# Order of leaf sums, scales and turns, and idle TensorE products, in a fused conditioned block of two layer pairs

## The chip, the cores and the metric

The kernel runs on one core of one Trainium2 chip. Its engines are TensorE (PE in the profile; its weight loads are PEld), VectorE (DVE), ScalarE (ACT), GpSimd (POOL) and SyncE (SP), which issues most DMAs. Each engine works through its own queue in program order and waits on semaphores for the others. The metric is the device time of one execution in microseconds (us). The kernel before takes 595.75 us, the median of three runs (595.74 to 597.34).

## The reference

x has 2 batches of 2048 rows of 512 columns, all float32. Cut to what matters:

```python
emb = silu(t) @ ada_w + ada_b
shift_msa, scale_msa, gate_msa, shift_mlp, scale_mlp, gate_mlp = split(emb, 6)
norm = ln(x) * (1 + scale_msa) + shift_msa
h = gelu(norm @ ssm_w1 + ssm_b1)            # 512 -> 512
x = x + gate_msa * (h @ ssm_w2 + ssm_b2)    # 512 -> 512
norm2 = ln(x) * (1 + scale_mlp) + shift_mlp
hf = gelu_tanh(norm2 @ ff_w1 + ff_b1)       # 512 -> 1024
x = x + gate_mlp * (hf @ ff_w2 + ff_b2)     # 1024 -> 512
```

ln takes mean and variance over the 512 columns. The shifts, scales and gates are one row per batch.

## The kernel before

The 4096 rows are cut into eight blocks of 512 rows, i = 0 to 7; four blocks make a batch. A block passes through four matrix products, named by their tiles: hA (first layer, `First`), oA (its residual, `residual`), hC (feed-forward layer, `Second`), oC (its residual, `residual_in_leaves` for i from 1 on). Everything is float32, in which a product of TensorE runs as two passes. A product of two matrices cut into quarters is made of seven quarter products instead of eight, from sums of quarters that VectorE and GpSimd form ahead (P1 to P7, taken in the order P1, P2, P6, P5, P7, P3, P4); hC from i=1 on takes 26 products from a table (`HK_P`), whose right operands are 20 forms of the normalised block, made by the list `HK_B` into the tile `forms`; and in oC some of the seven are split again into "leaves", seven rounds r = 0 to 6 of small products, whose operands are the leaf sums sums24, sums35 and sums7 of hC's output (`leaf_sums`, each four sums in the line L348). VectorE adds each round's result from PSUM into x (L795) before the banks are used two rounds on. "five" is true in all blocks but 1 and 4: then five of the seven go by leaves (P2, P3, P4, P5, P7) and P1 and P6 are plain; otherwise three do (P2, P3, P4).

The order of all work is written by hand. Each product takes a dictionary of hooks: `hook(hooks, places, ops)` puts operations behind a place, and they are emitted there, in the order of hooking. Places of hC are the numbers 0 to 25 of its products; places of hA and oA are P1 to P7; places of oC are P1 and P2 behind plain products (in a five block P2 lies behind the plain P6), and for a five block P6, P5, R2, P7, (R4, P3), P4 behind rounds 1, 2, 3, 4, 5, 6. In the others P1, P2, P6 lie behind the plain P1, P5, P6, and P5, R2, P7, R4, P3, P4 behind rounds 1 to 6. Where an operation stands among the hooks sets its place in its engine's queue, not a time.

A norm (`Norm`; n1 ahead of hA, n2 ahead of hC) goes through these steps: `stats` (VectorE, L508); `scales` (L513), which makes 1/sqrt and the scaled mean of four values a row in eight small steps on GpSimd, or, with on_dve, the first two there (L517, L519, a power of -0.5) and four on VectorE (L525 to L528); `normal` (ScalarE, L549); `turn` (VectorE, L560, transposes within 32 by 32); `move` (16 DMAs of 64 KB, L569, on SP or on SP and ScalarE's queue by halves); `moved`, the modulation by scale and shift (ScalarE, L592, or another engine, L594); then the forms (L870).

While hC of block i runs, x of block i+1 is loaded a second time (`load_x(i + 1)`), since its first copy was normalised in place; its buffer is that of a block whose store must be done. The loop at L1216 emits for block i: hC_i; oA of i+1; oC_i with n2 of i+1 hooked into it; then hA of i+2. `nxt` and `nx2` say that i+1 and i+2 exist, `last` is i = 7. In block 4, `leaf_fold` holds sums that remake the leaf weights for the second batch.

At the start five idle products of 512 columns (L1026) run on the identity while the first loads land, then rows_of(0) (L275), 32 small products for the shift rows, once ada_0 has landed, and rows_of(1) once ada_1 has; then 16 transposes of the first normalised block (L578) and their modulation (L592, L594), and the first layer of block 0.

Of the kernel before, what the change touches and what calls it, by code (L numbers as in the profile page):

```python
# [83 lines left out]
HK_B = [  # L84
    (23, '-', 4, 6),
    (22, '-', 0, 23),
    (21, '+', 1, 3),
    (20, '-', 21, 22),
    (19, '-', 7, 21),
    (18, '-', 5, 21),  # L90
    (17, '+', 3, 23),
    (16, '-', 18, 23),
# [48 lines left out]
def kernel(  # L141
# [16 lines left out]
    nc = tc.nc  # L158
    P = 128
# [4 lines left out]
    C = 4  # L164
# [22 lines left out]
    IDLE = 5  # L187
# [5 lines left out]
    ROWS = R_FB1 + KH  # L193
    def big_tile(name):
        return big.tile([P, KD, D], F32, tag="big", name=name)
# [3 lines left out]
    def load_x(i, pieces=1):  # L199
        xs[i] = big_tile(f"x_{i}")  # L200
        for s in range(pieces):
            c = slice(s * C // pieces, (s + 1) * C // pieces)
            nc.sync.dma_start(out=xs[i][:, c, :], in_=x_blk[i][:, c, :])
# [29 lines left out]
    rows = brows[:ROWS, 2, :P]  # L233
# [5 lines left out]
    ident = const.tile([P, P], F32, tag="ident", name="ident")  # L239
# [29 lines left out]
    def rows_of(g):  # L269

        pa = ps_g.tile([P, D], F32, tag="x", name=f"pada_{g}")
        w = ada[g].rearrange("p k (n m q) -> p k m n q", n=KD, q=G)
        for k in range(KD):
            for m in range(P // G):
                nc.tensor.matmul(  # L275
                    pa[m * G : (m + 1) * G, :P],
                    silu[:, k, :],
                    w[:, k, m],
                    start=(k == 0),
                    stop=(k == KD - 1),  # L280
                    tile_position=(0, m * G),
                    skip_group_check=True,
                )
        return pa

    def modulation(g0, part):

        g = g0 + part
        pa = rows_of(g)
        turned = pa[:, P : 2 * P]  # L290
        nc.vector.transpose(turned, pa[:, :P])
        turned = turned.rearrange("p (n q) -> p n q", n=KD)
        m = const.tile([P, KD, B], F32, tag=f"mod_{g0}_{part}", name=f"mod_{g0}_{part}")
        bias = colsT[:, R_ADA + g * KD : R_ADA + (g + 1) * KD]
        nc.vector.tensor_tensor(m, turned[:, :, :B], bias.unsqueeze(2).to_broadcast([P, KD, B]), ALU.add)
        mods[g0, part] = m
# [80 lines left out]
    def weight_of_first(name, w_sb):  # L377

        K, M = w_sb.shape[1], w_sb.shape[2]
        tile_s = const.tile([P, 3, K // 2, M // 2], F32, tag=f"{name}_s", name=f"{name}_s")  # L380
        s = thirds(tile_s)
        lo, hi = w_sb[:, : K // 2, :], w_sb[:, K // 2 :, :]
        q = quarters(lo, hi, slice(0, M // 2), slice(M // 2, M))
        return first_operands(q, s), sums_of_first(q, s, nc.gpsimd), tile_s
# [28 lines left out]
    def leaves_of_weight(w_sb, s, engs):  # L413


        def views(w):
            v = w.rearrange("p (h k) (q e d) -> p h k q e d", h=2, e=2, d=P)
            return {f"{h + 1}{e + 1}": v[:, h, :, :, e, :] for h in range(2) for e in range(2)}

        lo, hi = w_sb[:, : w_sb.shape[1] // 2, :], w_sb[:, w_sb.shape[1] // 2 :, :]  # L420
        q23, t23 = views(hi), thirds(pair_t)
        o23 = second_operands(q23, t23)
        ops = {p: {n: v[:, :, j, :] for n, v in o23.items()} for j, p in enumerate(("P2", "P3"))}
        sums = {"P23": sums_of_second(q23, t23, engs["P23"])}
        for j, (p, w) in enumerate((("P4", s[:, 2]), ("P5", s[:, 0]), ("P7", lo[:, :, D // 2 :]))):
            q, t = {n: v[:, :, 0, :] for n, v in views(w).items()}, thirds(fw2_t[:, 2 + j])
            ops[p] = second_operands(q, t)
            sums[p] = sums_of_second(q, t, engs[p])
        return ops, sums
# [59 lines left out]
    def hook(hooks, places, ops):  # L489

        for n, op in enumerate(ops):
            hooks.setdefault(places[min(n, len(places) - 1)], []).append(op)
# [369 lines left out]
    def sums_of_registers(program, reg, engs):  # L862


        def op(n, d, f, a, b):
            eng = engs[n % len(engs)]
            if f == "n":
                nc.vector.scalar_tensor_tensor(reg[d], reg[a], -1.0, reg[b], ALU.mult, ALU.subtract)
            else:
                eng.tensor_tensor(reg[d], reg[a], reg[b], ALU.add if f == "+" else ALU.subtract)  # L870

        return [lambda z=(n,) + step: op(*z) for n, step in enumerate(program)]
# [128 lines left out]
    def run(ops):  # L1001
        for op in ops:
            op()
# [4 lines left out]
    n1 = {0: Norm(0, 1), 1: Norm(1, 1)}  # L1008
# [9 lines left out]
    pt = ps_t.tile([P, 512], F32, tag="t", name="rowsT")  # L1018
# [1 line left out]
    fb1T = colsT[:, R_FB1:ROWS]  # L1020

    idle = ps_g.tile([P, C, P], F32, tag="v", name="idle")
    for n in range(IDLE):
        if n == IDLE - 1:
            nc.tensor.transpose(pt[:, :ROWS], rows, ident[:ROWS, :ROWS])
        nc.tensor.matmul(  # L1026
            idle, ident, ident.unsqueeze(1).to_broadcast([P, C, P]), start=True, stop=True
        )

    run(n1[0].stats())  # L1030
    nc.vector.tensor_copy(colsT, pt[:, :ROWS])
# [18 lines left out]
    w1_ops, w1_sums, _ = weight_of_first("w1", w1_sb)  # L1050
    run(w1_sums)
    modulation(0, 0)
    for c in range(C):
        n1[0].normal(c, nc.vector if c % 2 else None, on_pe=True)
    modulation(0, 1)
# [14 lines left out]
    gb, hA = {2: b2_bc}, {}  # L1070
# [12 lines left out]
    hooks = {}  # L1083
# [12 lines left out]
    hooks = {}  # L1096
# [4 lines left out]
    n2 = {0: Norm(0, 2)}  # L1101
# [21 lines left out]
    hooks = {}  # L1123
# [19 lines left out]
    hooks = {}  # L1143
# [8 lines left out]
    turns = [lambda c=c: n1[2].turn(c) for c in range(C)]  # L1152
# [5 lines left out]
    hooks = {}  # L1158
# [25 lines left out]
    hooks = {}  # L1184
# [10 lines left out]
    hooks = {}  # L1195
# [7 lines left out]
    hooks = {}  # L1203
# [12 lines left out]
    for i in range(1, NBLK):  # L1216
        five = i % PER_B != (1 if i < PER_B else 0)
        nxt, nx2, last = i + 1 < NBLK, i + 2 < NBLK, i + 1 == NBLK
        hC = Second(i)
        hooks = {}  # L1220
        if i == 1:
            hook(hooks, range(0, 26), take(len(fa_sums)))
        if i == 1:
            engs = {"P23": nc.gpsimd, "P4": nc.gpsimd, "P5": nc.vector, "P7": nc.vector}
            leaf_wops, ops = leaves_of_weight(fw2_sb, fw2_s, engs)
# [6 lines left out]
            hook(hooks, (0, 1, 3, 5, 7), later)  # L1232
            later = []
        if nxt:
            hook(hooks, (0,), [lambda: load_x(i + 1)])
            hook(hooks, (1, 2, 3, 4), hA[i + 1].summed(nc.gpsimd))
        if nx2 and i > 1:
            hook(hooks, (5,) if five else (9,), [n1[i + 2].scales])
# [19 lines left out]
        hooks = {}  # L1258
        hook(hooks, EARLY, hC.summed(1, nc.gpsimd if nxt else nc.vector))
        engs = (nc.gpsimd, nc.gpsimd, nc.gpsimd if nx2 else nc.vector)  # L1260
        sums24, sums35, sums7 = hC.leaf_sums(nxt, nx2, five, engs)
        hook(hooks, ("P5",), sums24)
        if last or not five:
            hook(hooks, ("P7",), sums35)
        else:
            hook(hooks, ("P7",) if nx2 else ("P5", "P7", "P7", "P3"), sums7)
        if nxt:

# [11 lines left out]
        leaf_fold, fold = fold and fold[11:], None  # L1280

        hooks = {}
# [6 lines left out]
            hook(hooks, ("P2",), [lambda: apart_leaves(gb[5], nc.gpsimd)])  # L1289
        if nxt:  # L1290

            hook(hooks, ("P1",), [lambda: n2[i + 1].scales(on_dve=not nx2)])
            if five:
                hook(hooks, ("P1",), sums35)
            hook(hooks, ("P1",), [lambda c=c: n2[i + 1].normal(c) for c in range(C)])
            turns = (("P6",) if leaf_fold else ("P2",) if five else ("P2", "P2", "P6")) if nx2 else ("P1",)
            if leaf_fold:
                hook(hooks, ("P1", "P1", "P2", "P2"), leaf_fold)
            hook(hooks, turns, [lambda c=c: n2[i + 1].turn(c) for c in range(C)])
            hook(hooks, turns[-1:], [lambda: n2[i + 1].move((nc.sync, nc.scalar))])  # L1300
# [5 lines left out]
        if nx2:  # L1306
            hook(hooks, ("P1", "P2"), n1[i + 2].summed(nc.gpsimd))
        if nxt:
            moved = n2[i + 1].moved((None,) if nx2 else (None, nc.vector))
            hook(hooks, ("R2",) if nx2 else ("P5", "R2", "P5", "R2"), moved)  # L1310
        refold5 = (i + 1) % PER_B == 0 and nxt
        if not last and not refold5:
# [4 lines left out]
        if nxt:  # L1317
            late = {}

            def form(engs):  # L1320

                fb[i + 1] = n2[i + 1].registers()
                return sums_of_registers(HK_B, fb[i + 1], engs)

            if not nx2:

                def late_form(n):
                    if n == 0:
                        late["ops"] = form((nc.vector,) * 4 + (nc.gpsimd,) * 16)
                    late["ops"][n]()  # L1330

                hook(hooks, ("R2",), [lambda n=n: late_form(n) for n in range(len(HK_B))])

        residual_in_leaves(f"oC_{i}", i, hC, fw2_ops, leaf_wops, KH // 2, hooks, last, five)
        if refold5:
# [8 lines left out]
        if refold5:  # L1344
            take_gate(5, b)
            fw2_ops, fold = weight_of_second(fw2_sb, fw2_s, gate[5, b], (nc.vector,))
            leaf_wops, ops = leaves_of_weight(fw2_sb, fw2_s, dict.fromkeys(("P23", "P4", "P5", "P7"), nc.vector))
            fold += ops["P23"] + ops["P4"]
            later = ops["P5"] + ops["P7"]
        hooks = {}  # L1350
# [13 lines left out]
            unread_stats = st[2:] if refold5 else []  # L1364
            hook(hooks, ("P7", "P4") if refold5 else ("P5", "P7", "P3", "P4"), st[:2] if refold5 else st)
        if nx2:
            hA[i + 2] = First(i + 2, n1[i + 2].ops, hooks, on_act=("P6", "P5"))


# [43 lines left out]
```

## Time and profile before

| | us |
|---|---|
| runs | 595.74, 595.75, 597.34 |
| profiled execution, its own time | 597.37 |
| its span, first to last instruction | 595.2 |
| TensorE busy | 581.6 (98%), 3247 instructions |
| TensorE's weight loads busy | 517.2 (87%) |
| VectorE busy | 434.5 (73%) |
| GpSimd busy | 424.2 (71%) |
| ScalarE busy | 244.7 (41%) |
| mean granted TensorE clock | 0.994 of full |

A busy engine is one that executes; TensorE's weight loads lie beside its products. Where stages are named by time: block 0 up to 133, then per block hC, oA, oC and the next hA, some 69 us in all; hC_4 begins at 342.6, oC_4 at 377.4, hC_6 at 483.1, oC_6 at 517.6, hC_7 at 544.7, oC_7 at 567.2; TensorE ends at 590.6.

### The profile page before, as it was taken

To read this page: it belongs to the slowest core of one execution; us is meant where nothing else is said; L and a number is where in the kernel's file an instruction comes from. 1 tells how busy PE (TensorE), PEld (TensorE's weight loads), DVE (VectorE), ACT (ScalarE), POOL (GpSimd) and SP (SyncE) were. 2 spreads that over 40 slices of the span, in tenths; PEclk is the share of its full clock that TensorE was granted. 3 is DMA by queue.
4 is the path that set the end of the run, shared out by engine and by line. 5 is a ranking of instruction groups with operands and counts; after the bars stand their busy time and mean duration, and the time that the engine had idled before them with its cause. 6 is when DMAs were issued, how large, how long until landed. Compare 5 with 4: busy or idle time off the path is not lost.

```text
span 595.2 us, 9335 instructions
## 1 busy us (share of the span) xinstructions
PE 581.6 (98%) x3247; PEld 517.2 (87%) x3247; DVE 434.5 (73%) x784; ACT 244.7 (41%) x425; POOL 424.2 (71%) x503
## 2 busy tenths in 40 slices
PE   7999999999999999999999999999999999989996
PEld 4888888887889888998889988888889988879886
DVE  4879788996665685786757688756857636788686
ACT  2235357405632454444733457135554346112420
POOL 2676359999982958969697869948689773645470
PEclk9999999999999999999999999999999999989999
DMA  8990323302205303452034711144021500022002
GB/s 318 395 380 5 90 63 84 103 36 106 56 17 149 153 0 77 123 181 81 10 81 131 247 48 40 33 117 166 2 66 26 155 38 1 0 47 97 1 1 72
DMA packets 25243, 56.49 MB, mean 95 GB/s; under 512 B 4672, under 2 KB 5740, under 8 KB 23532
## 3 DMA queue, kind: packets, MB, share of 16 engines
q1 hardware_dynamic: 21472, 51.15, 26.6%
q10 hardware_dynamic: 3724, 4.75, 3.3%
q8 instruction: 26, 0.43, 0.3%
q14 instruction: 21, 0.17, 0.1%
HBM read 32.80 MB, written 8.40 MB: 69 GB/s over the span
## 4 chain that ended last, share of the span: by engine, by line
PE 78%; DVE 9%; POOL 5%; issue 3%; DMA 2%; ACT 1%; SPq 0%; DVEq 0%; POOLq 0%; ACTq 0%
PE py_hA L474 9%; PE px_hC L932 8%; PE py_oA L474 8%; PE pv_hC L932 7%; PE py_hC L932 7%; PE pl_oC_P_y L781 6%; PE py_oC L735 6%; PE pv_hA L474 4%; PE pl_oC_P_v L781 4%; PE pv_oA L474 4%; PE py_hC L474 2%; PE px_hA L474 2%; PE px_oA L474 2%; PE pl_oC_P_x L781 2%; DMA ada<-in_L_cond_ada_w_dram 2%
## 5 line engine op out<-in xcount | busy, mean ns | idle before, releaser
L348 POOL TENSOR_TENSOR hSC<-hClo,hChi 128x512 f32<-128x512 f32 (+1 forms) x17 | 20.6, 1215 | 40.3 <-ACT hChi L927 20.5
L508 DVE BATCH_NORM_STATS2 st<-x 128x6 f32<-128x512 f32 x64 | 43.3, 677 | 5.2 <-DMA x<-in_x_dram 5.0
L592 ACT ACTIVATE nT<-nT,mod,mod 128x512 f32<-128x512 f32 x30 | 22.0, 803 | 56.3 <-DMA nT<-blocks 42.4
L870 POOL TENSOR_TENSOR forms<-forms 128x256 f32<-128x256 f32 x55 | 41.4, 752 | 3.2
L932 PE MATMUL py_hC<-forms,fw 128*128 128x256 f32 x168 | 40.8, 379 | 0.0
L870 POOL TENSOR_TENSOR forms<-nT,forms 128x256 f32<-128x256 f32 x41 | 30.1, 757 | 13.6 <-DVE forms L870 13.1
L549 ACT ACTIVATE nT<-x,nmr,rstd 128x512 f32<-128x512 f32 x32 | 23.4, 803 | 39.7 <-POOL nmr L535 30.6
L949 DVE TENSOR_TENSOR hClo<-hClo,py_hC 128x512 f32<-128x512 f32 x42 | 28.5, 684 | 15.3 <-ACT hClo L946 9.5
L932 PEld LDWEIGHTS py_hC<-forms,fw 128*128 128x128 f32 x168 | 31.9, 190 | 4.4
L697 DVE TENSOR_TENSOR x<-py_oA,x 128x512 f32<-128x512 f32 x32 | 22.0, 687 | 18.1 <-PE py_oA L474 17.5
L795 DVE TENSOR_TENSOR x<-pl_oC_P_y,x 128x256 f32<-128x256 f32 (+1 forms) x76 | 28.0, 370 | 9.4 <-PE pl_oC_P_y L781 7.6
L735 PE MATMUL py_oC<-fw,hClo 128*128 128x256 f32 x144 | 33.6, 379 | 0.0
L592 ACT ACTIVATE x<-x,mod,mod 128x512 f32<-128x512 f32 x24 | 17.6, 802 | 38.8 <-DMA x<-blocks 38.8
L870 POOL TENSOR_TENSOR forms<-nT 128x256 f32<-128x256 f32 x12 | 9.1, 756 | 30.8 <-DMA x<-in_x_dram 18.8
L735 PEld LDWEIGHTS py_oC<-fw,hClo 128*128 128x128 f32 x144 | 26.8, 190 | 3.3
L949 DVE TENSOR_TENSOR hChi<-hChi,pv_hC 128x512 f32<-128x512 f32 x35 | 23.2, 680 | 7.0 <-PE pv_hC L932 6.9
L927 ACT ACTIVATE hClo<-hClo,colsT 128x256 f32<-128x256 f32 x56 | 25.3, 499 | 6.3 <-DVE hClo L949 6.0
L932 PE MATMUL px_hC<-forms,fw 128*128 128x256 f32 x112 | 27.6, 379 | 0.0
L474 PE MATMUL py_oA<-w,hA 128*128 128x256 f32 x112 | 26.5, 379 | 0.0
L946 ACT ACTIVATE hClo<-px_hC 128x512 f32<-128x512 f32 x21 | 12.5, 597 | 33.1 <-PE px_hC L932 22.3
L735 PE MATMUL py_oC<-fw_s,hSC 128*128 128x256 f32 x112 | 25.4, 380 | 0.6 <-DVE x L746 0.6
L927 ACT ACTIVATE hChi<-hChi,colsT 128x256 f32<-128x256 f32 x56 | 25.1, 496 | 1.9 <-DVE hChi L949 1.9
(330 smaller groups left out, 1750.5 us busy)
## 6 DMA issues: line engine op xcount, KB each, us to landing
x<-in_x_dram SPq DMA_DIRECT2D x13, 1024.0 KB
out_dram<-x SPq DMA_DIRECT2D x14, 512.0 KB
ada<-in_L_cond_ada_w_dram SPq DMA_DIRECT2D x6, 1024.0 KB
x<-blocks SPq DMA_DIRECT2D x96, 64.0 KB
nT<-blocks SPq DMA_DIRECT2D x72, 64.0 KB
fw<-in_L_cond_ff_w_dram SPq DMA_DIRECT2D x2, 2048.0 KB
nT<-blocks ACTq DMA_DIRECT2D x56, 64.0 KB
w<-in_L_cond_ssm_w_dram SPq DMA_DIRECT2D x3, 1024.0 KB
```

The lines of the kernel that those rows point to most:

```text
L474: nc.tensor.matmul(ps[b][j * apart][:, j, :], lhs(p, j, k), rhs(p, j, k), start=(fresh and j * (not apart) == 0 and k == 0), stop=(p in (" ...
L508: nc.vector.bn_stats(st, xs[self.i][:, c, :])
L549: nc.scalar.activation(t, x_c, AF.Identity, bias=self.nmr[:, c : c + 1], scale=self.rstd[:, c : c + 1])
L592: nc.scalar.activation(dst, src, AF.Identity, bias=shift, scale=scale)
L697: nc.vector.tensor_tensor(d, ps[BANK[p]][:, js], d, ALU.add)
L735: yield lambda j=j, k=k: nc.tensor.matmul(ps[BANK[p]][:, j, :], hops(p, j, k), wops[p][:, k, :], start=False, stop=(k == kdim - 1), skip_g ...
L781: nc.tensor.matmul(t[:, n, :], hops.leaves[p][f][:, k, :], leaf_wops[p][f][:, k, :], start=room not in started, stop=(f in ("P2", "P3", "P ...
L795: nc.vector.tensor_tensor(d, src, d, ALU.add)
L870: eng.tensor_tensor(reg[d], reg[a], reg[b], ALU.add if f == "+" else ALU.subtract)
L927: nc.scalar.activation(h, h, AF.Gelu_apprx_tanh, bias=fb1T[:, m : m + 1])
L932: nc.tensor.matmul(ps[b][:, j, :], fa[ra][:, j * P : (j + 1) * P], fb[rb].rearrange("p a (c q) -> p c a q", q=Q), start=(fresh and j == 0) ...
L949: nc.vector.tensor_tensor(dest(d), dest(d), ps[b], op)
```

## The change

Six edits in one diff. In the loop:

- **Leaf sums and scales.** In blocks 1 and 4 sums35 moves from P7 of oA to P1 of oC, behind the scales of the next norm. In block 6 the scales are made on GpSimd alone. In the last block sums35 is emitted ahead of sums24.
- **Turns.** In block 4 the four transposes and the 16 DMAs behind them move from P6 to P5 of oC; in block 6 from P1 to P2.
- **Modulation and forms of block 7** (emitted in block 6): two of the four modulations go from VectorE to GpSimd; the forms are hooked at P7 instead of R2, and VectorE makes six of the 20 instead of four.
- **Second load of x**: behind product 3 of hC instead of product 0.
- **First reads of hA**: in blocks 1 and 4 the first reads of P6 and P5 go from ScalarE to VectorE.

At the start the idle products get a helper, `warm`; one product of 128 columns is added behind the five, and three of 256 columns between rows_of(0) and rows_of(1).

```diff
@@ -1020,12 +1020,20 @@
     fb1T = colsT[:, R_FB1:ROWS]
 
     idle = ps_g.tile([P, C, P], F32, tag="v", name="idle")
-    for n in range(IDLE):
-        if n == IDLE - 1:
-            nc.tensor.transpose(pt[:, :ROWS], rows, ident[:ROWS, :ROWS])
-        nc.tensor.matmul(
-            idle, ident, ident.unsqueeze(1).to_broadcast([P, C, P]), start=True, stop=True
-        )
+    def warm(count, blocks=2):
+        for _ in range(count):
+            nc.tensor.matmul(
+                idle[:, :blocks],
+                ident,
+                ident.unsqueeze(1).to_broadcast([P, blocks, P]),
+                start=True,
+                stop=True,
+            )
+
+    warm(IDLE - 1, C)
+    nc.tensor.transpose(pt[:, :ROWS], rows, ident[:ROWS, :ROWS])
+    warm(1, C)
+    warm(1, 1)
 
     run(n1[0].stats())
     nc.vector.tensor_copy(colsT, pt[:, :ROWS])
@@ -1050,6 +1058,7 @@
     w1_ops, w1_sums, _ = weight_of_first("w1", w1_sb)
     run(w1_sums)
     modulation(0, 0)
+    warm(3)
     for c in range(C):
         n1[0].normal(c, nc.vector if c % 2 else None, on_pe=True)
     modulation(0, 1)
@@ -1232,7 +1241,7 @@
             hook(hooks, (0, 1, 3, 5, 7), later)
             later = []
         if nxt:
-            hook(hooks, (0,), [lambda: load_x(i + 1)])
+            hook(hooks, (3,), [lambda: load_x(i + 1)])
             hook(hooks, (1, 2, 3, 4), hA[i + 1].summed(nc.gpsimd))
         if nx2 and i > 1:
             hook(hooks, (5,) if five else (9,), [n1[i + 2].scales])
@@ -1259,10 +1268,10 @@
         hook(hooks, EARLY, hC.summed(1, nc.gpsimd if nxt else nc.vector))
         engs = (nc.gpsimd, nc.gpsimd, nc.gpsimd if nx2 else nc.vector)
         sums24, sums35, sums7 = hC.leaf_sums(nxt, nx2, five, engs)
+        if last:
+            hook(hooks, ("P5",), sums35)
         hook(hooks, ("P5",), sums24)
-        if last or not five:
-            hook(hooks, ("P7",), sums35)
-        else:
+        if five and not last:
             hook(hooks, ("P7",) if nx2 else ("P5", "P7", "P7", "P3"), sums7)
         if nxt:
 
@@ -1289,11 +1298,10 @@
             hook(hooks, ("P2",), [lambda: apart_leaves(gb[5], nc.gpsimd)])
         if nxt:
 
-            hook(hooks, ("P1",), [lambda: n2[i + 1].scales(on_dve=not nx2)])
-            if five:
-                hook(hooks, ("P1",), sums35)
+            hook(hooks, ("P1",), [lambda: n2[i + 1].scales()])
+            hook(hooks, ("P1",), sums35)
             hook(hooks, ("P1",), [lambda c=c: n2[i + 1].normal(c) for c in range(C)])
-            turns = (("P6",) if leaf_fold else ("P2",) if five else ("P2", "P2", "P6")) if nx2 else ("P1",)
+            turns = ("P5",) if leaf_fold else ("P2",) if five else ("P2", "P2", "P6")
             if leaf_fold:
                 hook(hooks, ("P1", "P1", "P2", "P2"), leaf_fold)
             hook(hooks, turns, [lambda c=c: n2[i + 1].turn(c) for c in range(C)])
@@ -1306,7 +1314,7 @@
         if nx2:
             hook(hooks, ("P1", "P2"), n1[i + 2].summed(nc.gpsimd))
         if nxt:
-            moved = n2[i + 1].moved((None,) if nx2 else (None, nc.vector))
+            moved = n2[i + 1].moved((None,) if nx2 else (None, nc.gpsimd))
             hook(hooks, ("R2",) if nx2 else ("P5", "R2", "P5", "R2"), moved)
         refold5 = (i + 1) % PER_B == 0 and nxt
         if not last and not refold5:
@@ -1326,10 +1334,10 @@
 
                 def late_form(n):
                     if n == 0:
-                        late["ops"] = form((nc.vector,) * 4 + (nc.gpsimd,) * 16)
+                        late["ops"] = form((nc.vector,) * 6 + (nc.gpsimd,) * 14)
                     late["ops"][n]()
 
-                hook(hooks, ("R2",), [lambda n=n: late_form(n) for n in range(len(HK_B))])
+                hook(hooks, ("P7",), [lambda n=n: late_form(n) for n in range(len(HK_B))])
 
         residual_in_leaves(f"oC_{i}", i, hC, fw2_ops, leaf_wops, KH // 2, hooks, last, five)
         if refold5:
@@ -1364,7 +1372,7 @@
             unread_stats = st[2:] if refold5 else []
             hook(hooks, ("P7", "P4") if refold5 else ("P5", "P7", "P3", "P4"), st[:2] if refold5 else st)
         if nx2:
-            hA[i + 2] = First(i + 2, n1[i + 2].ops, hooks, on_act=("P6", "P5"))
+            hA[i + 2] = First(i + 2, n1[i + 2].ops, hooks, on_act=("P6", "P5") if five else ())
 
 
 # ---- launch: one core; inputs and outputs as the reference has them ----
```

## The prediction

> **What bounds the kernel.** I read the busy table first (TensorE 98% of the 595.2 us span), then TensorE's waits, which say how little there is to win, then the granted clock in short windows around each wait, then the timeline of those places. TensorE's waits are these:
>
> ```profile
> PE pl_oC_P_y L781 <- DVE x L795: 3.6, 3, 2.5
> PE pada L275 <- DMA ada<-in_L_cond_ada_w_dram: 2.6, 2, 1.5
> ...
> PE px_hC L932 <- DVE hChi L949: 0.8, 1, 0.8
> PE py_oC L735 <- DVE x L746: 0.6, 1, 0.6
> ```
>
> So nothing but TensorE's own stops can be removed. The clock says that two of them cost more than their length:
>
> ```profile
> 13.60:15.00 1.40, 1.40 (x10) 1.40 (x8) 0.50 (x2) 0.28 (x1) 0.28 (x1) 0.50 1.05 386
> 529.00:531.60 2.60, 0.16 (x2) 0.01 (x1) 2.50 (x6) 1.43 (x3) 0.00 (x0) 0.91 0.00 0
> 531.60:533.00 1.40, 1.37 (x6) 1.40 (x7) 1.36 (x4) 0.00 (x0) 0.00 (x0) 0.50 0.41 91
> ```
>
> The eighth column is the granted clock (after the window, its length and five engines). After the stop of 1.52 us at 10.5 it is 0.60, 0.50 and 0.75 until 16.5; after the stop of 2.47 us in block 6 it is 0.50 from 531.6 to about 534.7. After the stops of 0.98 us (block 4), 0.79 us (block 1) and 0.57 us (last block) it stays 1.00.
>
> **Start: idle products.** Here the timeline reads:
>
> ```profile
> 9.38 1.08 PE L275 MATMUL pada<-ada,silu 128*32 128x128 f32 x32 [1.05 <-DMA ada<-in_L_cond_ada_w_dram]
> 11.98 1.66 PE L275 MATMUL pada<-ada,silu 128*32 128x128 f32 x32 [1.52 <-DMA ada<-in_L_cond_ada_w_dram]
> 13.57 3.01 PE L578 MATMUL pt<-ident,blocks 128*128 128x128 f32 x16
> 16.41 1.89 PE L474 MATMUL py_hA<-nT,w 128*128 128x256 f32 x8
> ```
>
> Three idle products of 256 columns are added behind the first group. One is two passes; eight passes take 1.73 us in the first layer, so six take 1.30 us, from 10.46 to 11.76, which ends before the load at 11.98. The lone 128-column one at 8.33 lies in the wait to 9.38. At half clock the six would take 2.60 us and make the second group 1.08 us late, but the clock there is still 1.00. What they buy: the second group 1.66 to 1.08 (as the first), and the transposes at the rate of block 1 (8 in 1.04 us). The eighth then ends near 14.1, VectorE's modulation (0.81 us) near 15.1, and the first product starts near 15.2 instead of 16.41: 1.2 us. The GpSimd sums of w1 (14.72 to 20.24) and the loads that follow do not move with it; w2's row loads may take some back. I take **1.1**, ends 0 and 1.5 (0.58 and 0.93, all of both).
>
> The Trainium skill, "TensorE: Matmul & The Clock Gate", Part 1, lets the clock fall only after an idle window of some 3.4 us. By that rule neither stop would cost clock, the idle products would buy 0 and the sum below would be 1.1 us smaller. The rows above disagree: 1.52 us, with a thin group of small products before it, was enough.
>
> **Block 4 (i=4): scales ahead of sums35, turns from P6 to P5.**
>
> ```profile
> 385.81 0.51 POOL L517 TENSOR_SCALAR ve<-mv 128x4 f32<-128x4 f32 x1
> ...
> 390.06 2.83 DVE L560 STREAM_TRANSPOSE blocks<-nT 128x512 f32<-128x512 f32 x4 [1.37 <-ACT nT L549]
> ...
> 393.34 1.58 PE L781 MATMUL pl_oC_P_y<-fw_t,forms 128*128 128x128 f32 x12 [0.98 <-DVE x L795]
> ```
>
> The statistics were ready at 380.73; the scales stood behind sums35 (four of 0.73 to 0.91). VectorE then waits 1.37 us for the normalised rows and turns them (2.83 us) before the adds of leaf round 0, for which TensorE waits. Moved, the scales start near 382.6 and end near 385.9, sums35 follows until 388.8 (wanted by round 2, near 391.3), and the adds of rounds 0 and 1 run as their leaves end. The stop goes: 0.98, and 0.24 of slow restart (1.58 for 12 where 1.34 is usual). Price: the turns start near 391.6, so the 16 moving DMAs are issued 1.5 us later (394.45), and ScalarE's modulation comes 7.1 us behind them as in three blocks (181.47 to 188.47, 392.92 to 400.07, 531.20 to 538.21). The forms then start 404.6 instead of 403.1; the first feed-forward product wants the fourth of them, near 407.7, at 413. That cover is 5 us, so nothing. The load of x_7 now stands ahead of the moves on SP; its buffer's earlier contents were last read near 377, and no transfer runs from 386 to 392, so it goes early. If it didn't, the moves would wait behind 1 MB (2.7 us at the first stage's 390 GB/s), still inside the cover. I take **1.1**, ends 0.5 and 1.2. Block 1 has no such stop (its scales wait for statistics, 172.09), so 0.
>
> ScalarE's two first reads in the first layer go to VectorE in blocks 1 and 4: 0.69 us each where VectorE idles 2.4 us. Next user is TensorE's third read of that bank, 1 us later: 0.
>
> **Block 6 (i=6), the largest.**
>
> ```profile
> 522.46 1.04 POOL L519 TENSOR_TENSOR r<-ve,minus_half 128x4 f32<-128x4 f32 x1
> ...
> 526.14 1.19 DVE L528 SCALAR_TENSOR_TENSOR nmr<-mv,rstd 128x4 f32<-128x4 f32 x1
> ...
> 528.35 2.82 DVE L560 STREAM_TRANSPOSE blocks<-nT 128x512 f32<-128x512 f32 x4 [1.02 <-ACT nT L549]
> ...
> 531.63 2.05 PE L781 MATMUL pl_oC_P_y<-fw_t,leaves 128*128 128x128 f32 x8 [2.47 <-DVE x L795]
> ...
> 540.33 0.42 DVE L870 TENSOR_TENSOR forms<-nT 128x256 f32<-128x256 f32 x1
> ...
> 544.73 1.03 PE L932 MATMUL py_hC<-forms,fw_s 128*128 128x256 f32 x4
> ```
>
> VectorE's tiny scale steps take 1.1 to 1.2 us each while GpSimd sums beside them, and the turns at P1 stand ahead of round 0's adds. With all scales on GpSimd, root to last step take 2.77 us (386.40 to 389.17), so they end at 525.2, not 527.3. Turns, now behind round 0's adds, run from 526.1 to 528.95, moves are issued 2.2 us earlier and land near 536.05. Round 2 starts at 529.0; five rounds of 2.23 end at 540.15 instead of 544.73: 4.6 us, the stop and the slow clock.
>
> What is late next: the forms. Two modulations go to GpSimd, an operation with no row there. Bounds: 0.56 us (one-input affine select, 128 columns in 0.29, of which 0.2 is what 4 columns cost, scaled to 512) and 1.27 (two-input sum of that size). I take the middle, 0.9: done at 537.9. VectorE, free at 537.25 after round 4, waits for them, then forms six pieces of 0.42 us, slowed by about 0.5 where GpSimd sums beside them: to 541.0. Behind these in its queue stand the adds of round 5 (1.6 us), and the second feed-forward product needs the bank that they read: 542.6, where it was 545.59. So 3.0 of the 4.6 stay. At 0.56 the gain is 3.6, at 1.27 it is 2.2. The eleventh form, wanted by the fourth product at 544.3, comes near 544.0. I take **3.0**, ends 0.5 (1.27 and a slow clock of 1.7) and 4.6.
>
> The Trainium skill, "GPSIMD Engine Reference", 4.1 Engine selection, calls one-input work on GpSimd roughly line rate. An estimate from that page (512 elements at its 1.03 cycles and 1.2 GHz, with 0.2 us fixed) is 0.64 us; the sum would be 0.5 us larger. No run here shows it yet.
>
> **Last block.** sums35 ahead of sums24 makes GpSimd wait until VectorE's four sums are done; two of these took 1.75 us beside GpSimd and 0.69 alone, so the read behind them comes 2 us earlier and the stop of 0.57 goes. But sums24's second result, wanted by round 2 at 578.8, comes after six GpSimd sums from 571.05: 578.7 to 579.8. I take **0.2**, ends -0.5 and 0.6.
>
> **x three products later.** SP issues it when its buffer's store has landed (406.07, 3 us behind the store's issue), whatever product it is written at; only the small gate load passes it. 0; at best the 0.8 us stop of block 1.
>
> **Sum.** 1.1 + 1.1 + 3.0 + 0.2 = 5.4 us. The profiled execution took 597.37 us (span 595.2 and 2.2 around it): 592.0. The three runs are 595.74, 595.75 and 597.34; the profile belongs to the upper kind. The 1.6 us between them is about what one slow-clock stretch costs, and since these go, I expect one kind near 592.0; if the 1.6 lies elsewhere, the lower kind would be 590.4.
>
> **Rivals.** (1) The new wait at block 7's second product, about 1.5 us, again halves the clock: 1.7 more, 593.7. For it: 1.52 at the start did; against it: 0.98 did not. Chance 0.17. (2) Less wait: fast GpSimd modulation, or the lower kind of run, about 590.3: 0.17. (3) It doesn't do what it says: start and last block return nothing and block 6 nets 0.5, so 597.37 - 1.6 = 595.8: 0.08. (4) Slower: GpSimd's modulation with two per-partition scalars is a slow program, as its power step is (1.04 us for 4 columns where a sum takes 0.20). Block 6 breaks even at 2.5 us each; above 3.7 it eats the 2.4 us of the other terms. At 4.5 the second product starts at 549.7, 4.1 late: 597.37 + 1.7 = 599.1. 0.08. The forecast itself, 592.0 within about 1.3: 0.50.
>
> **How the numbers follow.** A difference of 0.3% (1.8 us) is about what a measurement can tell from none. Faster (under 594.0) holds the forecast, (2) and most of (1): 0.77; same 0.14, from (3) and the rest of (1); slower 0.09. The range takes in (1), (2) and the bounds until (3): 589.5 to 595.6.
>
> **What would show it.** Right: clock 1.00 from 10 to 17 and in block 6; first-layer product near 15.2; no wait of TensorE in leaf rounds of blocks 4 and 6; a new wait at block 7's second product on VectorE's leaf adds. Wrong: GpSimd's modulation over 1.3 us, a clock of 0.5 in block 7, or TensorE waiting for the GpSimd leaf sums in the last block.

## The result, and the profile after

The changed kernel takes 590.28 us, the median of four runs (589.62, 589.76, 590.80, 591.35); the kernel before, beside it, 595.75 us (595.63 to 597.34). The ratio is 0.9904, 95% interval 0.9880 to 0.9928: about 1% faster. The profiled execution of the changed kernel took 591.35 us with a span of 589.2; against the profiled one of before (595.2) that is 6.0 us of span.

TensorE's waits in the changed kernel, all of them, in the columns engine and line, what it waited for, us in total, times, longest:

```profile
PE rowsT L1034 <- DMA fw_t<-in_L_cond_ff_b_dram: 2.4, 1, 2.4
PE idle L1025 <- POOL ident masks.py:199: 1.3, 1, 1.3
PE pv_hC L932 <- POOL forms L870: 1.2, 1, 1.2
PE pl_oC_P_y L781 <- POOL forms L348: 0.6, 1, 0.6
PE pada L275 <- DMA ada<-in_L_cond_ada_w_dram: 0.3, 1, 0.3
```

The four waits shown before, on VectorE's leaf adds (3.6 us in three), on the second ada load, on hChi and on L746, are gone. Two on GpSimd are new: `pv_hC`, block 7's second product, and `pl_oC_P_y`, round 2 of the last block. `rowsT` waits for the first load: in this execution that product starts at 9.33, in the profile of before at 7.02, so nothing at the start came sooner here. (The profile of before has the half clock at its start, the one of after this late load; the two nearly cancel in the first row of the table.)

How far TensorE had come tells where the 6.0 us lie. The starts of hC in each block, and of the last product of all:

| stretch (TensorE) | before, us | after, us | saved |
|---|---|---|---|
| start of span to hC_1 | 133.04 | 133.10 | -0.06 |
| hC_1 to hC_2 | 71.21 | 69.83 | 1.38 |
| hC_2 to hC_4 | 138.32 | 138.32 | 0.00 |
| hC_4 to hC_5 | 71.36 | 70.09 | 1.27 |
| hC_5 to hC_6 | 69.16 | 69.16 | 0.00 |
| hC_6 to hC_7 | 61.64 | 57.22 | 4.42 |
| hC_7 to its third product | 1.73 | 3.19 | -1.46 |
| third product to the last of all | 43.65 | 43.65 | 0.00 |
| last product to end of span | 5.09 | 4.64 | 0.45 |

So block 6 nets 2.96 and block 4 1.27, about as forecast; block 1, forecast at 0, returned 1.38, and the start, forecast at 1.1, returned nothing in this pair of executions. No run explains the last row.

The new wait of block 7, in the timeline of the changed kernel (start, length, engine and line, what, count, the idle time before it and what ended it):

```profile
533.80 1.53 POOL L594 TENSOR_SCALAR nT<-nT,mod,mod 128x512 f32<-128x512 f32 x2 [6.14 <-DMA nT<-blocks]
535.36 0.43 DVE L870 TENSOR_TENSOR forms<-nT 128x256 f32<-128x256 f32 x1 [0.88 <-POOL nT L594]
...
536.17 0.95 DVE L870 TENSOR_TENSOR forms<-nT 128x256 f32<-128x256 f32 x1
...
537.49 0.75 DVE L870 TENSOR_TENSOR forms<-nT,forms 128x256 f32<-128x256 f32 x2
538.16 1.60 DVE L795 TENSOR_TENSOR x<-pl_oC_P_v,x 128x256 f32<-128x256 f32 x4
...
539.97 1.10 PE L932 MATMUL pv_hC<-nT,fw_s 128*128 128x256 f32 x4 [1.15 <-POOL forms L870]
```

GpSimd's two modulations take 0.76 us each. VectorE waits 0.88 us for them, makes six forms (one slowed from 0.42 to 0.95 beside a GpSimd form), then the four adds of round 5, which end at 539.76; the second product starts 0.21 us behind them. The last line names a GpSimd form as what ended the wait; that is tried below.

### The profile page after: what moved, and what is told of

It reads as the page before. It is cut to its first block, busy times and chain, and to the rows that moved or that the text cites. A ratio compares the mean times of both kernels' runs of the same rounds, so it can differ in the third digit from the quotient of the medians.

```text
span 589.2 us, 9347 instructions
## 1 busy us (share of the span) xinstructions
PE 579.3 (98%) x3255; PEld 515.4 (87%) x3255; DVE 432.1 (73%) x784; ACT 241.4 (41%) x417; POOL 424.2 (72%) x509
## 4 chain that ended last, share of the span: by engine, by line
PE 89%; DVE 3%; DMA 2%; POOL 2%; issue 1%; ACTq 1%; ACT 0%; SPq 0%; POOLq 0%; DVEq 0%
PE px_hC L932 10%; PE py_hA L474 9%; PE py_oA L474 9%; PE pv_hC L932 8%; PE py_hC L932 8%; PE py_oC L735 7%; PE pl_oC_P_y L781 6%; PE pv_hA L474 4%; PE pv_oA L474 4%; PE pl_oC_P_v L781 4%; PE py_hC L474 2%; PE px_hA L474 2%; PE px_oA L474 2%; PE py_oC L474 2%; DMA ada<-in_L_cond_ada_w_dram 2%; PE pl_oC_P_x L781 2%
## 5 line engine op out<-in xcount | busy, mean ns | idle before, releaser
L870 POOL TENSOR_TENSOR forms<-nT,forms 128x256 f32<-128x256 f32 x39 | 28.7, 755 | 1.0 <-DVE forms L870 0.5
L517 POOL TENSOR_SCALAR ve<-mv 128x4 f32<-128x4 f32 x16 | 3.8, 240 | 34.3 <-DVE mv L509 26.1
```

## The experiments

Twelve kernels ran, in three sets, each beside the kernel before (medians 595.81, 595.78 and 595.77 us). Ratios are to that kernel, with 95% intervals. The edits are shown cut to what matters.

### The load of x, alone

```diff
-            hook(hooks, (0,), [lambda: load_x(i + 1)])
+            hook(hooks, (3,), [lambda: load_x(i + 1)])   # x_at3; (2,) in x_at2
```

> The kernel before with the second load of x behind product 3 and nothing else. Theory A (buffers): a buffer is given out at the first write in program order. Product 3 is the first whose result is written into hClo, so a load ahead of it takes the free buffer and leaves ScalarE's first copy into hClo the one whose store is still running (138.66, 2.23 us after its last work, TensorE stopped 0.79). Behind it they change places: ScalarE copies at once, the load waits. Expected: the stop in block 1 is gone, the load issued 2 us later, 1.4 us gained, as between the two traces from product 5 on. Rival B (traffic): the load merely stands aside for the store, and any later place helps by as much as it is later. Rival C: the 1.4 us came from another edit, and this kernel equals before.

> The kernel before with the second load of x behind product 2, one product short of the first write of hClo. Theory A (buffers): nothing changes, ScalarE's copy still waits for the store and TensorE still stops 0.8 us in block 1; same time as before. Rival B (traffic): two thirds of what product 3 gives, some 0.9 us.

Behind product 3: 594.38 us (12 runs), ratio 0.9979 (0.9970 to 0.9989), hC_1 to hC_2 in 69.82 us. Behind product 2: 595.85 us (11 runs), ratio 1.0004 (0.9995 to 1.0014), 71.16 us, as before. One product decides. The timelines of block 1's first products, x_at2 and then x_at3:

```profile
133.79 0.37 SPq L203 DMA_DIRECT2D x<-in_x_dram  x1
...
136.95 0.60 ACT L946 ACTIVATE hClo<-px_hC 128x512 f32<-128x512 f32 x1 [2.18 <-DMA out_dram<-x]
138.32 2.32 PE L932 MATMUL px_hC<-forms,fw_s 128*128 128x256 f32 x8 [0.74 <-DVE hChi L949]
```

```profile
136.28 0.60 ACT L946 ACTIVATE hClo<-px_hC 128x512 f32<-128x512 f32 x1 [0.33 <-PE px_hC L932]
...
137.18 0.34 SPq L203 DMA_DIRECT2D x<-in_x_dram  x1
...
138.61 1.89 PE L932 MATMUL px_hC<-forms,fw_s 128*128 128x256 f32 x8
```

What differs is who waits for the store of the earlier x. The tile `hClo` is first written by ScalarE behind product 3. Emitted before that write, the load takes the free buffer and `hClo` gets the one whose store is still under way: ScalarE waits 2.18 us for a store (`out_dram<-x`), VectorE's add comes late, and TensorE stops 0.74 us and restarts slowly (2.32 for what else takes 1.89). Emitted after it, the two swap buffers: ScalarE's wait falls to 0.33, and the load waits 2.2 us for the store on SP, where no product needs it. ScalarE's copy at 136.28 comes before that store has landed, which shows the swap.

The swap brings a second thing with it: the load no longer runs beside the store. The store has landed 4.6 us behind block 1's first product in x_at3 (137.18 against 132.57) and 5.4 us behind it in x_at2 (136.79 against 131.37). x_at2 can't refute the rival of the traffic: its load is later in the program but not in time, since the stores stand ahead of it in SP's queue (issued 2.4 us behind the first product, in the profile of before too, 135.45 against 133.04). How much of the gain the quicker store alone would give was not tested.

### The idle products: alone, and taken from the changed kernel

The two hunks at the start, alone on the kernel before (warm_only), and the changed kernel without them (after_no_warm).

> The kernel before with the idle products alone. Theory: the granted clock stays 1.00 from the first shift rows to the first layer; counted from the start of the first shift rows' group to the first product of block 0, 5.9 us (11.10 to 16.55 was 5.5 in the changed kernel) instead of 7.0 (9.38 to 16.41), and the gain of 1.1 to 1.6 us is still there at block 1. Rival: the sums of w1 on GpSimd and the later loads hold the first layer, and by 30 us nothing is left: time as before within 0.3 us.

> The changed kernel with the idle products as in the kernel before. Theory: the start with a half clock is a matter of chance (before, some third of the runs lie 1.4 us above the others, and with the idle products alone none do), so this kernel has two kinds of run again, the lower at the changed kernel's lower time (589.7) and the upper 1.4 us above. Rival: the idle products are worth 1.1 us or more in every run, and all runs lie that much above the changed kernel.

warm_only: 595.95 us (11 runs, 595.66 to 596.30), ratio 0.9997 (0.9988 to 1.0005). after_no_warm: 589.66 us (589.43, 589.45, 589.65, 589.67, 591.35, 592.41), ratio 0.9899 (0.9880 to 0.9919). The median run gains nothing from them. The reason is in x_at2, which has no idle products in that stop. Its first products, and its granted clock in two windows (the stretch, its length, five engines, then the clock):

```profile
9.38 1.08 PE L275 MATMUL pada<-ada,silu 128*32 128x128 f32 x32 [0.83 <-DMA ada<-in_L_cond_ada_w_dram]
12.00 1.08 PE L275 MATMUL pada<-ada,silu 128*32 128x128 f32 x32 [1.54 <-DMA ada<-in_L_cond_ada_w_dram]
13.01 1.97 PE L578 MATMUL pt<-ident,blocks 128*128 128x128 f32 x16
14.82 1.52 PE L474 MATMUL py_hA<-nT,w 128*128 128x256 f32 x6
```

```profile
11.90:13.50 1.60, 1.50 (x36) 1.30 (x37) 0.39 (x2) 0.20 (x1) 0.00 (x0) 1.00 1.05 388
13.50:15.00 1.50, 1.50 (x15) 1.47 (x14) 0.97 (x2) 1.19 (x2) 0.26 (x1) 1.00 1.04 384
```

The same stop (1.54 us; 1.52 in the profile of before) and no fall of the clock: the first layer begins at 14.82, not 16.41. Three of six profiles without idle products other than that of before (x_at3, block6_only, after_no_warm) had the half clock there and began the first layer at 16.06 to 17.24; the other three (x_at2, block4_only, last_only) had 1.00 and began at 14.73 to 14.82. It is a matter of the execution, and the profile of before was one with the half clock. With the idle products the stop is filled, as in warm_only:

```profile
10.26 1.56 PE L1025 MATMUL idle<-ident 128*128 128x256 f32 x6
11.86 1.08 PE L275 MATMUL pada<-ada,silu 128*32 128x128 f32 x32
14.68 1.95 PE L474 MATMUL py_hA<-nT,w 128*128 128x256 f32 x8
```

In all seven profiles with them the clock is 1.00 from 8 to 18 us. The runs agree. Of the 60 runs of the kernel before in the three sets, 17 lie above 596.8 us and the rest between 595.2 and 596.5; of warm_only's 11 none lies above 596.3. Among the kernels that have the edits of block 6 too, the mean clock of a run is 0.998 or more in all 27 runs with idle products, and 0.997 or less in 6 of the 11 without (block6_only, after_no_warm). So the idle products do keep the clock up; this is worth about 1.4 us in an execution that would have had the half clock, and nothing in the median, since most runs of before don't have it. In those warm_only is some 0.2 us slower (595.95 against 595.72, the median of the 28 runs of before at a mean clock of 1.000). The changed kernel's runs of 590.8 and 591.35 have a mean clock of 1.00; the latter is the profiled one, with the first load 2.3 us late.

warm_only says more, of block 6. There the clock stays at 1.00 behind the stop of 2.48 us (0.50 in the profile of before), and hC_6 to hC_7 still takes 61.64 us. Its windows, then VectorE's timeline (its first add of round 0, its last form, its first add of round 4), then TensorE's round 6 in warm_only and in the profile of before:

```profile
529.80:531.00 1.20, 0.87 (x8) 0.90 (x9) 1.06 (x4) 0.00 (x0) 0.00 (x0) 1.00 0.10 24
531.00:533.60 2.60, 2.60 (x26) 2.60 (x25) 2.36 (x7) 0.00 (x0) 0.00 (x0) 1.00 0.89 203
```

```profile
529.60 0.39 DVE L795 TENSOR_TENSOR x<-pl_oC_P_y,x 128x256 f32<-128x256 f32 x1
...
540.07 0.42 DVE L870 TENSOR_TENSOR forms<-forms 128x256 f32<-128x256 f32 x1
540.42 0.42 DVE L795 TENSOR_TENSOR x<-pl_oC_P_y,x 128x256 f32<-128x256 f32 x1
```

```profile
540.89 0.71 PE L781 MATMUL pl_oC_P_y<-fw_t,hChi 128*128 128x128 f32 x4 [1.47 <-DVE x L795]
```

```profile
542.39 0.71 PE L781 MATMUL pl_oC_P_y<-fw_t,hChi 128*128 128x128 f32 x4 [0.19 <-DVE x L795]
```

What a full clock saved in rounds 2 to 5 is waited for at round 6 (1.47 us, 0.19 in the profile of before), for VectorE's adds of round 4, which stand behind its modulations and four forms. VectorE's queue holds the rounds: from its first add of round 0 to that of round 4 it takes 10.82 us at the full clock (529.60 to 540.42) and as much beside the half clock (531.10 to 541.92 in the profile of before). So the half clock lay beside that chain and cost nothing. The runs say the same: 14 of the 60 of before have a mean clock of 0.995 or 0.996, which in x_at2's profile is this half clock alone, and their median is 595.71, that of the 28 at 1.000 is 595.72; the 16 at 0.997 (in block6_only's profile the half clock of the start alone) have a median of 597.10. Only in x_at3's profile, where the clock fell somewhat earlier, did VectorE once wait for TensorE (0.46 us), and the stage took 61.99 us.

### Block 6, block 4 and the last block, each alone on the kernel before

```diff
 # block6_only
-            hook(hooks, ("P1",), [lambda: n2[i + 1].scales(on_dve=not nx2)])
+            hook(hooks, ("P1",), [lambda: n2[i + 1].scales()])
-            turns = (...) if nx2 else ("P1",)
+            turns = (...) if nx2 else ("P2",)
-            moved = n2[i + 1].moved((None,) if nx2 else (None, nc.vector))
+            moved = n2[i + 1].moved((None,) if nx2 else (None, nc.gpsimd))
-                        late["ops"] = form((nc.vector,) * 4 + (nc.gpsimd,) * 16)
+                        late["ops"] = form((nc.vector,) * 6 + (nc.gpsimd,) * 14)
-                hook(hooks, ("R2",), [lambda n=n: late_form(n) for n in range(len(HK_B))])
+                hook(hooks, ("P7",), [lambda n=n: late_form(n) for n in range(len(HK_B))])
 # block4_only
-        if last or not five:
+        if last:
-        else:
+        elif five:
-            if five:
-                hook(hooks, ("P1",), sums35)
+            hook(hooks, ("P1",), sums35)
-            turns = (("P6",) if leaf_fold else ...) if nx2 else ("P1",)
+            turns = (("P5",) if leaf_fold else ...) if nx2 else ("P1",)
 # last_only
+        if last:
+            hook(hooks, ("P5",), sums35)
         hook(hooks, ("P5",), sums24)
-        if last or not five:
+        if not five:
-        else:
+        elif not last:
```

> The kernel before with the edits of block 6 alone (scales on GpSimd, turns at P2, two modulations on GpSimd, forms at P7 with six on VectorE). Theory: the stop of 2.47 us and the half clock behind it go (4.4 us to the first product of block 7), 1.5 us come back at its second product: 3.0 us net, about 592.8 from 595.75, or 594.4 from the upper kind of run. Rival: if the half clock behind the stop is not there in the lower kind of run, only 1.3 us net.

> The kernel before with sums35 behind the scales in blocks 1 and 4 and the turns of block 4 at P5, nothing else. Theory: the stop of 0.98 us ahead of leaf round 2 of block 4 goes, 1.2 us from the start of hC_4 to that of hC_5 (71.36 to 70.1, as between the two traces), block 1 unchanged; 594.6 from 595.8. Rival: the later moves or the load ahead of them give part of it back at the forms of block 5, under 0.5 us net.

> The kernel before with sums35 ahead of sums24 in the last block alone. Theory: VectorE's sums run without GpSimd beside them (0.69 instead of 1.75 us), the stop of 0.57 at P6 goes, and a wait of about as much for sums24's second sum comes at round 2: the last product at the same time within 0.2 us. In the changed kernel the time from the start of the last products to the span's end is 0.45 us shorter; if that is this edit's, the time falls by 0.4 us; rival: it is not, and the time is that of before within 0.2 us.

block6_only: 593.90 us (5 runs), ratio 0.9959 (0.9946 to 0.9972); hC_6 to hC_7 57.25 us, then the wait of 1.1 us at block 7's second product. Four of its five runs (593.66 to 594.03) have a mean clock of 0.997, as the runs of before near 597.1; the fifth, at 1.000, took 592.47, where before takes 595.7. Like with like that is 3.2 us both times, more than the ratio says: the theory holds, and the rival of 1.3 us is refuted. block4_only: 594.42 us (12 runs), ratio 0.9979 (0.9969 to 0.9989); hC_4 to hC_5 70.14 us, the stop of 1.0 gone; the changed kernel's 70.09, which also has ScalarE's two reads moved, leaves 0.05 for those. last_only: 595.74 us (12 runs), ratio 0.9996 (0.9985 to 1.0007); the stop of 0.57 us at P6 is replaced by one of 0.6 in round 2, and hC_7 to the last product takes 45.37 us where it took 45.38.

### Who holds block 7's second product

The changed kernel with four forms on VectorE, as before, in place of six:

```diff
-                        late["ops"] = form((nc.vector,) * 6 + (nc.gpsimd,) * 14)
+                        late["ops"] = form((nc.vector,) * 4 + (nc.gpsimd,) * 16)
```

> The changed kernel with four forms of block 7 on VectorE and 16 on GpSimd, as before, still at P7. Theory: the second product of block 7 waits for VectorE's adds of leaf round 5, which stand behind the six forms; with four they come 0.75 us earlier and that product starts so much earlier, but the eleventh form on GpSimd, wanted two products later, comes 1 us later, so the wait moves there and the sum is 0 to 1 us worse. Rival, as the profile names the releaser: the second product waits for forms of GpSimd; then its wait grows by 1 us itself.

590.10 us (4 runs), ratio 0.9895 (0.9879 to 0.9912). Its TensorE timeline in block 7:

```profile
536.18 1.03 PE L932 MATMUL py_hC<-forms,fw_s 128*128 128x256 f32 x4
537.45 1.10 PE L932 MATMUL pv_hC<-nT,fw_s 128*128 128x256 f32 x4 [0.23 <-PE py_hC L932]
538.39 1.03 PE L932 MATMUL px_hC<-forms,fw 128*128 128x256 f32 x4
540.84 1.13 PE L932 MATMUL px_hC<-forms,fw 128*128 128x256 f32 x4 [1.43 <-POOL forms L870]
```

With two forms fewer ahead of VectorE's adds these end at 537.24 and the second product comes 1.27 us behind the first, not 2.25. In both kernels it starts 0.21 us behind the end of the adds (539.76 to 539.97, 537.24 to 537.45), and `HK_P` gives it as right operand a register (3) that no form writes. So it waits for the adds; GpSimd has more to do here and the wait shrank, which refutes the releaser that the profile names. The wait moves on: the fourth product, 4.66 us behind the first (4.05 in the changed kernel, 2.59 in block 1, where nothing is late), now waits for GpSimd's forms. Six on VectorE is the better of the two by 0.6 us of trace; the medians (590.10 and 590.28, not from the same set) don't show it.

### Versions beyond the change

```diff
 # leaf_inter: the changed kernel, last block in turns
-        if last:
-            hook(hooks, ("P5",), sums35)
-        hook(hooks, ("P5",), sums24)
+        hook(hooks, ("P5",), sums35[:2] + sums24[:2] + sums35[2:] + sums24[2:] if last else sums24)
 # best1: leaf_inter, block 6's second GpSimd modulation on VectorE
-            moved = n2[i + 1].moved((None,) if nx2 else (None, nc.gpsimd))
-            hook(hooks, ("R2",) if nx2 else ("P5", "R2", "P5", "R2"), moved)
+            moved = n2[i + 1].moved((None,) if nx2 else (None, nc.gpsimd, None, nc.vector))
+            hook(hooks, ("R2",) if nx2 else ("P5", "R2", "P5", "P7"), moved)
 # best2: best1, block 6's moves from three queues
-                    engs[m % len(engs)].dma_start(
+                    engs[(a * C + m if len(engs) == 3 else m) % len(engs)].dma_start(
-            hook(hooks, turns[-1:], [lambda: n2[i + 1].move((nc.sync, nc.scalar))])
+            hook(hooks, turns[-1:], [lambda: n2[i + 1].move((nc.sync, nc.scalar) if nx2 else (nc.sync, nc.scalar, nc.gpsimd))])
```

> The changed kernel, with the last block's GpSimd sums in turns: two of sums35, two of sums24, the rest of sums35, the rest of sums24. My theory is that the last block returned nothing because the stop of 0.57 us went from one leaf round to round 2, whose sum now stands behind six sums of the other list; in turns each sum comes before its round: both stops go and the time falls by 0.5 to 0.8 us against the changed kernel (590.28 to about 589.6). The rival is that GpSimd is simply short of time there (busy beside VectorE): then one of the two stops stays at 0.5 us or more and the time is that of the changed kernel.

> leaf_inter, and in block 6 the four modulations go to ScalarE, GpSimd, ScalarE and VectorE (were ScalarE and GpSimd in turn), VectorE's after the adds of round 3 (P7) in place of GpSimd's second. My theory: block 7's second product waits for VectorE's adds behind its forms, and the forms begin when GpSimd's second modulation ends (0.76 us each); with one of them on VectorE the last is done about 0.3 us sooner and the second product's wait of 1.15 us shrinks by that: about 0.3 us off leaf_inter. The rival: VectorE loses as much by doing it as it wins by starting sooner (0.4 us more work in its queue): no change, within 0.2 us of leaf_inter.

> best1, and in block 6 the 16 moving transfers are issued from three queues (SyncE, ScalarE and GpSimd in turn) in place of two. Each issue takes about 0.66 us on its queue, 8 on each of two; with three, 5 or 6 each, some 1.5 us less. My theory is that the landing of these moves bounds the modulation and thereby the forms, so the modulation starts up to 1.2 us sooner, the second product's wait goes, and 0.5 to 1.0 us come off best1. The rival: GpSimd's issues hold up its leaf sums and forms (behind them in its queue), so the eleventh form, wanted by the fourth product, is later by as much: same as best1 or slower by up to 2 us, with a wait of TensorE on GpSimd in its place.

> The changed kernel itself, beside the three others on one chip, for their comparison and a second profile of it: 589.4 to 590.3 us for most executions, the wait of about 1.1 us at block 7's second product and of 0.57 us in round 2 of the last block as in its first profile; its start varies with the clock granted there.

| kernel | median us (runs) | ratio, 95% | hC_6 to last product, us |
|---|---|---|---|
| after_again | 589.74 (5) | 0.9893 (0.9878 to 0.9909) | 103.87 |
| leaf_inter | 588.90 (5) | 0.9884 (0.9865 to 0.9902) | 103.22 |
| best1 | 589.08 (5) | 0.9890 (0.9869 to 0.9910) | 102.95 |
| best2 | 588.56 (4) | 0.9871 (0.9853 to 0.9890) | 103.26 |

leaf_inter does what was expected of it: both stops are gone, hC_7 to the last product takes 46.00 us (46.80 in after_again; 0.65 us less counted from hC_6), and the median is 0.84 us lower, at the upper end of the forecast. One of its five runs lies at 590.69, and the two ratios' intervals overlap, so the gain rests on the trace more than on the medians. Round 2 of the last block, in the changed kernel and then in leaf_inter:

```profile
572.56 0.61 PE L781 MATMUL pl_oC_P_x<-fw,hClo 128*128 128x128 f32 x4
573.74 1.16 PE L781 MATMUL pl_oC_P_y<-fw_t,forms 128*128 128x128 f32 x8 [0.57 <-POOL forms L348]
```

```profile
570.94 0.61 PE L781 MATMUL pl_oC_P_x<-fw,hClo 128*128 128x128 f32 x4
571.38 1.06 PE L781 MATMUL pl_oC_P_y<-fw_t,forms 128*128 128x128 f32 x8
```

The product follows 0.44 us behind the one before it, no longer 1.18. GpSimd does the same eight sums; only their order was wrong.

best1 does what it should in the trace (forms begin 0.26 us sooner, the second product too, hC_6 to the last product 0.27 shorter); its runs scatter more than that. The theory of best2 is refuted by its trace. The issues and ScalarE's modulation in best1, then in best2:

```profile
524.76 5.49 ACTq L569 DMA_DIRECT2D nT<-blocks  x8
...
531.84 1.52 ACT L592 ACTIVATE nT<-nT,mod,mod 128x512 f32<-128x512 f32 x2 [7.86 <-DVE x L795]
```

```profile
524.78 3.39 ACTq L569 DMA_DIRECT2D nT<-blocks  x5
526.04 2.71 POOL L569 DMA_DIRECT2D nT<-blocks  x5
...
532.15 1.52 ACT L592 ACTIVATE nT<-nT,mod,mod 128x512 f32<-128x512 f32 x2 [8.15 <-DMA nT<-blocks]
```

SP and ScalarE are done issuing 1.5 to 2.1 us sooner, but GpSimd starts its five only behind its sums, at 526.04, and is done at 528.75; they take a median of 3.5 us from issue to landing. The modulation starts 0.3 us later. best2's low median is not shown to be a gain of this edit: its stage is the longer one in the trace.

The best kernels here are leaf_inter and what was built on it, 588.6 to 589.1 us, which these runs don't order among themselves.

## Why the prediction was near, and where it failed

The time fell in the range, but 1.7 us below the 592.0 that was thought likeliest, at the price of the second rival (590.3). Two mechanisms were right (blocks 4 and 6); that the total lies so near the second rival's is luck, as the next paragraphs show.

**Sum.** Of the steps of 5.4 us, blocks 4 and 6 were right; the idle products (1.1) and the last block (0.2) returned nothing in the median run, and x, put at 0, returned 1.38. By the parts alone (one minus each ratio, times 595.8): x 1.25, block 4 1.25, block 6 2.4, last block 0.2, idle products 0.2; the intervals reach 0.5 to 0.8 us to either side, and block 6's figure is too small for the reason given above. By the trace: 1.38, 1.27, 2.96, 0, and for the idle products nothing in an execution without the half clock. The trace's sum is 5.6; the medians differ by 5.5.

**"Since these go, I expect one kind near 592.0"** failed. The two stretches of half clock were read as costs of the kernel. The one at the start comes in some executions only, 17 of 60, and is worth about 1.4 us between the two kinds of run; the one in block 6 was hidden behind VectorE's queue. The sum was taken from the upper kind, 597.37. For that kind the start was about right; what the sum lacks there is x (1.38) and the end of the span (0.45): 597.37 - 1.4 - 1.27 - 2.96 - 1.38 - 0.45 = 589.9, an estimate from the rows above. The sentence's alternative, "if the 1.6 lies elsewhere, the lower kind would be 590.4", meets the median by luck: the 1.6 did lie at the start, so the lower kind couldn't gain the 1.1 of the idle products, and x's 1.38 stood in for it.

**"x three products later. 0"** failed, by the step "SP issues it when its buffer's store has landed, whatever product it is written at". The buffer isn't fixed: the product at which the load stands decides which buffer it gets, and whether ScalarE or SP waits. The "0.8 us stop" named as the best case was 1.38 us, 0.95 to the next start (138.22 to 140.04 against 138.28 to 139.15) and 0.44 of slow restart.

**Block 4** was right: 1.1 forecast, 1.27 measured. The modulation came 7.15 us behind the moves (393.08 to 400.23; 7.1 forecast), and no product waited for it.

**Block 6** was right in size and mechanism, 3.0 forecast and 2.96 measured: rounds 4.42 us shorter (4.6 forecast), and 1.46 given back at the second product (1.6 forecast), for VectorE's adds behind its forms, and the eleventh form in time for the fourth product. GpSimd's modulation was 0.76 us, not 0.9. The prediction's estimate from the Trainium skill, "GPSIMD Engine Reference" (4.1, with the cycles of its 3.1), 0.64 us, was as far off on the other side. The step "the slow clock" as part of the 4.6 was wrong: VectorE's queue, not the clock, had held the rounds, and the edits took work out of it and brought its adds forward.

**Last block**: 0.2 forecast, 0 measured. The order of GpSimd's sums gave the stop back where the text said it might, at round 2. TensorE waiting for GpSimd's leaf sums in the last block was one of the prediction's own signs of being wrong, and it came.

**Rivals.** The half clock behind block 7's new wait (rival 1) didn't come: the clock is 1.00 from 535.3 to 546. Rival 4 fell with the 0.76 us. Against the rule of the Trainium skill, "TensorE: Matmul & The Clock Gate", Part 1, that the clock falls after an idle window of some 3.4 us, stand the half clocks after 1.52 and 2.47 us. The same section says that the window in which activity is counted runs free, and that the number of slow products at a kernel's start varies from run to run for that reason. The starts without idle products vary too, four profiles with the half clock and three without; no run here shows the window.

**Open.** The last store lands 3.2 to 3.3 us behind its issue in all kernels with the loop's edits together, and 3.5 to 3.7 us in all with one part or none: the 0.45 us at the end of the span. No run says why.

## What to carry to other kernels

Before a stretch of slow clock is priced, compare executions with and without it (here the mean clock of each run sorted them): a slow engine that lies beside the chain that binds costs nothing, and one profile may show an accident. Where a transfer is only moved in program order, ask which buffer it will be given and who then waits for that buffer's last reader; one place in the order was worth 1.4 us here. Where one engine makes the operands of two consumers, order its pieces by the consumers' turns, not list by list.

## What the runs showed of the hardware that was not expected

- The granted clock after the same stop of 1.5 us was 0.50 in four profiles and 1.00 in three of the same start; in the seven where idle products fill that stop it was 1.00.
- A one-input GpSimd operation with two per-partition scalars took 0.76 us for 128x512 float32, where a two-input sum of that size takes 1.27.
- Five 64 KB moves issued by GpSimd took 2.71 us of its queue, 0.54 each, and SP's and ScalarE's issues in the same stretch 0.62 to 0.69 each; with fewer issues a queue the rows landed no sooner.
